# A graph network's adjacency matrix loaded in place in 1 MB transfers, its small loads in the same queue, and two pairs' first products in step

## The chip, the cores and the metric

The kernel runs on one core of a Trainium2 chip. The metric is the device time of one execution in microseconds; the kernel before takes 1300.35 us (median of 3 runs, 1299.11 to 1302.89). Engines: PE multiplies matrices, PEld loads its weights, DVE and ACT work on vectors, Pool (GpSimd) does small vector work and issues transfers, SP issues transfers. "Clock" is the share of full speed that PE was granted. Where a comparison matters it is over several executions; the two kernels' runs of one comparison alternate on one chip.

## The reference

```python
# x (8, 2048, 64), adj (2048, 2048); four layers, each x + layer(relu(layernorm(x)))
h = jnp.maximum(_layernorm(x, axis=-1), 0.0)
x = x + _L0_gnn_ref(h, adj, L0_gnn_embedding, L0_gnn_weight, L0_gnn_bias)
# ...
# _L0_gnn_ref: As = [I, A, 2 A A - I]; every A_k @ h goes through weights made from the embedding
w = jnp.einsum('nd,dkio->nkio', embedding, weight)
b = jnp.einsum('nd,do->no', embedding, bias)
# ...
x_g = jnp.einsum('knm,bmc->bnkc', A_stack, x)
out = jnp.einsum('bnki,nkio->bno', x_g, w)
return out + b
```

adj is 0 or one over the row's count, so the kernel multiplies with its signs and scales the product by a row of values taken from its diagonal (`crow`).

## The kernel before

The batch is worked in four pairs of 64 columns. The change touches the opening of layer 0. There adj comes row block by row block (16 blocks of 128 rows, "rows" from here on, 1 MB each); ACT writes the sign into `BT`, which stays in SBUF as the operand of all later products. Meanwhile the first products of pair 0 (`banks[0]`, 8 matmuls for each row) and pair 1 (`banks[1]`, 6 for each row) are accumulated. h is split into a rounded half `H` and a remainder `L`.

```python
def load_adj(m, behind):
    for nb in range(NB):                       # 4 pieces of 256 KB for each row
        part_ = slice(nb * 512, (nb + 1) * 512)
        st = prop.tile([P, 512], F32, name="st", bufs=6)
        loads.append(nc.sync.dma_start(st, adj[m * P:(m + 1) * P, part_]))
        if nb == m // 4:                       # the diagonal, picked by DVE from the staging tile
            junk = prop.tile([P, P], U8, name="junk")
            nc.vector.scalar_tensor_tensor(junk, st[...], 1.0, ident, ..., accum_out=cols[:, m, :])
        with tc.issue_after(behind.ins) if behind else nullcontext():
            nc.scalar.activation(BT[:, m, part_], st, AF.Sign)
# ... norm of one tile of x: DVE mean, z; ACT square; DVE var; Pool rstd; DVE z; ACT H; DVE L
        rstd = small.tile([P, 8], F32, name="rstd", bufs=3)
        powers.append(nc.gpsimd.tensor_tensor(rstd, var, mhalf, op=ALU.pow))
# ...
    for m in range(NCH):
        # ... tick(): the next tile's norm
        load_adj(m, copies[i - 1] if i else None)
        if len(x01) < len(norm_order):
            load_x01()                         # x, 256-byte pieces, on SP
        # ...
        last = step(0, m, banks[0])
        # ...
        while done < (m - 3 if m < 12 else 2 * m - 14):   # pair 1 three rows behind
            with tc.issue_after(last.ins):
                step(1, done, banks[1])
            done += 1
```

`issue_after` sets an instruction's place in the order of its engine; it adds no wait of its own.

## Time and profile before

| | before |
|---|---|
| time, median of 3 | 1300.35 us |
| profiled execution: span, clock | 1295.8 us, 0.979 |
| first product | 13.8 us |
| interleaved products end | 95.8 us |
| first `y` product (the next stage) | 115.2 us |
| PE busy | 95% of the span |

The prediction below shows the lines that carry its reading. Two more are needed for comparison. They are the busy time of the kernel before in two stretches of the opening: bounds in us, length, then busy us and number of instructions for PE, PEld, DVE, ACT and Pool, then clock, busy share of the transfer engines and GB/s.

```profile
30.00:38.00 8.00, 2.45 (x4) 1.01 (x4) 2.68 (x6) 2.09 (x4) 5.24 (x5) 0.50 0.77 241
38.00:47.00 9.00, 7.55 (x18) 5.15 (x18) 6.06 (x16) 5.47 (x10) 2.87 (x3) 0.57 0.57 187
```

PE ran 4 and 18 matmuls there in 8 and 9 us, at half clock, while the transfer engines were 77% and 57% busy.

### The profile page before, as it was taken

The page shows a single profiled execution, that of the slowest core. Times are in us where ns is not written, and L with a number is a line of the kernel's source. Part 1 is how long each engine was busy: PE and PEld are TensorE (multiplying, and loading weights), DVE is VectorE, ACT ScalarE, POOL GpSimd, SP SyncE. Part 2 cuts the span into 40 slices and gives each one's busy share as a digit, 9 for nine tenths or more (in the row PEclk, how much of TensorE's full clock was granted, in tenths as well). Part 3 has the DMA queues.
Part 4 walks back from the last instruction along what each step waited for, and adds up shares of the span by engine and source line. Part 5 has one row for each costly group of instructions (what it writes and reads, how often), then busy time and mean ns, then how long its engine had stood idle before and what let it go on. Part 6 is the DMA issues. An engine that isn't in the chain of part 4 may idle for free.

```text
span 1295.8 us, 15644 instructions
## 1 busy us (share of the span) xinstructions
PE 1230.5 (95%) x5702; PEld 865.2 (67%) x5702; DVE 750.2 (58%) x1937; ACT 188.6 (15%) x313; POOL 224.6 (17%) x228
## 2 busy tenths in 40 slices
PE   3799999899999999999999999999999999989994
PEld 2476555455585556655558887878878878878883
DVE  5325887777747775357764435535644544566664
ACT  4541001000010000000011121112111211111110
POOL 4210111111121111011101024004201400332222
PEclk8799999999999999989999999999999999999997
DMA  9793334322343322123237535443653463433322
GB/s 252 227 240 114 86 94 111 93 73 63 95 104 82 81 78 68 35 55 86 58 83 174 107 90 158 115 93 106 159 118 90 139 130 94 151 102 106 97 67 52
DMA packets 149882, 140.11 MB, mean 108 GB/s; under 512 B 99892, under 2 KB 101940, under 8 KB 149796
## 3 DMA queue, kind: packets, MB, share of 16 engines
q1 hardware_dynamic: 137780, 106.54, 32.1%
q0 software_dynamic: 9904, 31.96, 8.7%
q8 instruction: 47, 0.77, 0.3%
q10 hardware_dynamic: 2112, 0.52, 0.2%
q14 instruction: 39, 0.32, 0.1%
HBM read 94.87 MB, written 35.73 MB: 101 GB/s over the span
## 4 chain that ended last, share of the span: by engine, by line
PE 77%; DMA 6%; DVE 6%; issue 6%; POOL 2%; ACT 1%; SPq 1%; ACTq 0%; POOLq 0%; DVEq 0%
PE bv L217 33%; PE y L580 22%; PE bn L523 4%; PE ph L742 3%; DMA st<-in_adj_dram 2%; PE bv_2b L217 2%; PE bv_3b L217 2%; DMA hb<-hs 2%; POOL rstd L169 1%; PE bv_1b L217 1%; PE bv_0a L217 1%; PE bn_u L523 1%; PE pt L229 1%; PE bv_0b L217 1%; DVE acc L589 1%
## 5 line engine op out<-in xcount | busy, mean ns | idle before, releaser
L217 PE MATMUL bv<-BT,H 128*128 128x512 f32 x1024 | 426.7, 417 | 0.0
L217 PE MATMUL bv<-BT,L 128*128 128x512 f32 x1024 | 401.3, 392 | 0.0
L217 PEld LDWEIGHTS bv<-BT,H 128*128 128x128 f32 x1024 | 192.9, 188 | 47.9 <-issue 11.5
L217 PEld LDWEIGHTS bv<-BT,L 128*128 128x128 f32 x1024 | 193.0, 188 | 47.5 <-issue 11.5
L589 DVE SCALAR_TENSOR_TENSOR acc<-y,emb,acc 128x128 f32<-128x128 f32 x512 | 176.3, 344 | 69.2 <-PE y L580 68.4
L580 PE MATMUL y<-wt,t0T 64*128 64x512 f32 x512 | 145.7, 611 | 9.2 <-DVE odd L589 9.2
L589 DVE SCALAR_TENSOR_TENSOR odd<-y,emb,odd 128x128 f32<-128x128 f32 x448 | 153.5, 343 | 0.0
L169 POOL TENSOR_TENSOR rstd<-var,mhalf 128x8 f32<-128x8 f32 x64 | 106.1, 1660 | 197.1 <-DVE var L167 191.6
L209 DVE TENSOR_TENSOR g<-bv,crow 128x512 f32<-128x512 f32 x48 | 33.2, 692 | 182.4 <-PE bv L217 182.4
L163 ACT ACTIVATE sq<-z 128x512 f32<-128x512 f32 x64 | 40.4, 631 | 404.9 <-DVE z L159 392.8
L580 PEld LDWEIGHTS y<-wt,t0T 64*128 64x128 f32 x512 | 46.8, 186 | 72.3 <-issue 66.5
L560 POOL TENSOR_TENSOR acc<-acc,wl 128x512 f32<-128x512 f32 x16 | 21.0, 1314 | 295.2 <-DVE z L159 294.0
L561 POOL DMA_DIRECT2D xs<-acc x32 | 18.0, 562 | 284.3 <-DVE acc L597 233.7
L580 PE MATMUL y<-wt,t1T 64*128 64x512 f32 x256 | 67.0, 589 | 0.0
L172 DVE SCALAR_TENSOR_TENSOR z<-z,rstd 128x512 f32<-128x512 f32 x64 | 44.7, 703 | 35.5 <-POOL rstd L169 35.5
L523 PEld LDWEIGHTS bn<-wl,g 128*128 128x128 f32 x384 | 49.4, 191 | 6.3 <-ACT g L747 3.1
L166 DVE TENSOR_REDUCE var<-sq 128x8 f32<-128x512 f32 x64 | 43.5, 680 | 16.1 <-ACT sq L163 16.1
L523 PE MATMUL bn<-wl,g 128*128 128x128 f32 x384 | 51.2, 276 | 0.7 <-ACT H L204 0.4
L689 DVE SCALAR_TENSOR_TENSOR junk<-mt,cols,st 128x512 uint8<-128x512 bf16 x64 | 49.2, 769 | 0.8 <-DMA mt<-MD 0.3
L580 PEld LDWEIGHTS y<-wt,t1T 64*128 64x128 f32 x256 | 27.6, 187 | 27.4 <-issue 27.1
L747 ACT ACTIVATE g<-g,b1s 128x512 f32<-128x512 f32 x32 | 23.2, 724 | 139.3 <-DVE g L746 139.3
L159 DVE TENSOR_TENSOR z<-acc,mean 128x512 f32<-128x512 f32 x56 | 38.3, 691 | 6.6 <-DMA hs<-z 5.0
(208 smaller groups left out, 1694.2 us busy)
## 6 DMA issues: line engine op xcount, KB each, us to landing
st<-in_adj_dram SPq DMA_DIRECT2D x128, 256.0 KB, 4.1
crow<-crowD SPq DMA_DIRECT2D x64, 256.0 KB, 3.3
hs<-z POOLq DMA_DIRECT2D x48, 256.0 KB, 2.9
hb<-hs SPq DMA_DIRECT2D x40, 256.0 KB, 3.3
xs<-acc POOLq DMA_DIRECT2D x32, 256.0 KB, 2.4
MD<-BT POOLq DMA_DIRECT2D x16, 512.0 KB, 5.1
acc<-xs SPq DMA_DIRECT2D x32, 256.0 KB, 3.5
acc<-in_x_dram SPq DMA_DIRECT2D x48, 128.0 KB, 3.7
```

What stands on the lines that cost most here:

```text
L159: nc.vector.tensor_tensor(g, groups(xt), mean[:, :, None].to_broadcast([P, 8, C]), op=ALU.subtract)
L163: nc.scalar.activation(sq, z, AF.Square)
L166: nc.vector.tensor_reduce(var, groups(sq), axis=AX.X, op=ALU.add)
L169: powers.append(nc.gpsimd.tensor_tensor(rstd, var, mhalf, op=ALU.pow))
L172: nc.vector.scalar_tensor_tensor(groups(h), g, 0.0, rstd[:, :, None].to_broadcast([P, 8, C]), op0=ALU.max, op1=ALU.mult)
L209: ahead.append(nc.vector.tensor_tensor(out, ps, crow, op=ALU.mult))
L217: nc.tensor.matmul(ps, hl[m // 4][i][:, m % 4, :], BT[:, m, nb * 512:(nb + 1) * 512], start=(m == 0 and i == 0), stop=(m == NCH - 1 and i ...
L523: nc.tensor.matmul(ps[:, t, :], fT[:, t * P:(t + 1) * P], wmat, start=True, stop=True)
L580: nc.tensor.matmul(y[:, bb, :], terms[k][hs_, ts], wt[hs_, k, dg * 512:(dg + 1) * 512], start=(k == 0), stop=(k == K - 1),)
L589: last = nc.vector.scalar_tensor_tensor(xj, yd, ec, old, op0=ALU.mult, op1=ALU.add)
L689: nc.vector.scalar_tensor_tensor(junk, mt, cols[:, i, :], st, op0=ALU.mult, op1=ALU.not_equal, accum_out=bad[:, i, q:q + 1],)
L742: fill[12] = lambda: nc.tensor.matmul(ph, w1v2 if s else w1vT, gT[nb], start=True, stop=True)
```

## The change

The intent: the rows go as 16 transfers of 1 MB straight into `BT`, and the sign is taken in place, so no staging buffer holds the queue. Loading into `BT` must go by Pool's queue (it rounds while it copies). x and four blocks of diagonals (`dg`) go by the same queue, so that Pool's order says what comes first; stores of h go to SP. Pair 1 stays one row behind pair 0. The bias products move behind the steps. The diff also loads the weights before the first `y`, moves the first transpose of `t0` into a product and reorders the norms.

```diff
-    def load_adj(m, behind):
-        for nb in range(NB):
-            part_ = slice(nb * 512, (nb + 1) * 512)
-            st = prop.tile([P, 512], F32, name="st", bufs=6)
-            loads.append(nc.sync.dma_start(st, adj[m * P:(m + 1) * P, part_]))
...
+    def load_dg(q):
+        loads.append(nc.gpsimd.dma_start(dg[q], bass.AP(
+            tensor=adj.tensor, offset=adj.offset + 4 * q * (P * N + P),
+            ap=[[N, P], [P * N + P, 4], [1, P]],
+        )))
...
+    def load_adj(m):
+        loads.append(nc.gpsimd.dma_start(BT[:, m, :], adj[m * P:(m + 1) * P, :]))
+
+    def pool_loads(behind, what):
+
+        order.append(behind)
+        for f, i in what:
+            with tc.issue_after(order[-1].ins):
+                f(i)
+            order.append(loads[-1])
+
+    def signs(m, behind=None):
+        for hf in range(2):
+            part_ = slice(hf * (N // 2), (hf + 1) * (N // 2))
             with tc.issue_after(behind.ins) if behind else nullcontext():
-                nc.scalar.activation(BT[:, m, part_], st, AF.Sign)
+                nc.scalar.activation(BT[:, m, part_], BTf[:, m, part_], AF.Sign)
...
+    pool_loads(order[0], ((row, 0), (lx, 2), (row, 1), (lx, 3), (row, 2)))
+    tick()
+    tick()
+    plan = {
+        0: (0, ((lx, 4),)), 1: (1, ((row, 3), (lx, 5), (row, 4))),
+        2: (2, ((lx, 6), (row, 5), (lx, 7))), 3: (3, ((row, 6), (row, 7), (dia, 0), (dia, 1))),
+        4: (4, ((row, 8), (row, 9))), 6: (5, ((row, 10), (row, 11), (dia, 2), (dia, 3))),
+        8: (6, ((row, 12), (row, 13))), 10: (7, ((row, 14), (row, 15))),
+    }
     for m in range(NCH):
...
+            pool_loads(powers[plan[m][0]], plan[m][1])
...
+        signs(m, squares[m] if m in (0, 2, 3) else copies[...])
         last = step(0, m, banks[0])
...
+                last = step(1, m - 1, banks[1])
```

`plan`: row 3 and later stand on Pool behind a given rstd operation (`lx` is x of one tile, `dia` a block of diagonals).

More of the change, by code (lines that the diff above doesn't have):

```diff
@@ L112, in uniform_path @@
     mhalf = consts.tile([P, 8], F32, name="mhalf")
-    nc.vector.memset(mhalf, -0.5)
+    order = [nc.gpsimd.memset(mhalf, -0.5)]
     def part(nb):
@@ L125, in fill_x @@
             for bb in range(2):
-                queue.dma_start(
+                ld = queue.dma_start(
                     acc[:, :, bb * C:(bb + 1) * C],
@@ L129, in fill_x @@
                 )
+            return ld
         else:
@@ L148, in uniform_path @@
     pending = []
-    powers = []
+    powers, firsts, squares, lows, stored = [], [], [], [], []
     ahead = []
@@ L158, in norm_stages @@
         nc.vector.tensor_scalar(mean, mean, 1.0 / C, None, op0=ALU.mult)
-        nc.vector.tensor_tensor(
+        firsts.append(nc.vector.tensor_tensor(
             g, groups(xt), mean[:, :, None].to_broadcast([P, 8, C]), op=ALU.subtract
-        )
+        ))
         sq = block("sq", f"sq_{name}", 1)
-        nc.scalar.activation(sq, z, AF.Square)
+        squares.append(nc.scalar.activation(sq, z, AF.Square))
         yield
@@ L197, in uniform_path, with halves @@
     copies = []
-    def halves(src, name, pool=None):
+    def halves(src, name, pool=None, later=None):
         pool, bufs = (work, 6) if pool is None else (pool, 4)
@@ L204, in halves, with rest @@
         copies.append(nc.scalar.copy(Hq, src))
-        nc.vector.tensor_tensor(Lq, src, Hq.bitcast(F32), op=ALU.subtract)
+        def rest():
+            lows.append(nc.vector.tensor_tensor(Lq, src, Hq.bitcast(F32), op=ALU.subtract))
+        rest() if later is None else later.append(rest)
         return Hq, Lq
@@ L249, in done @@
         def done(z):
-            nc.gpsimd.dma_start(hs[p][:, part(nb), :], z)
+            stored.append(
+                (nc.gpsimd if xt is None else nc.sync).dma_start(hs[p][:, part(nb), :], z)
+            )
             if also is not None:
@@ L254, in norm_0 @@
         norm_relu(load_x(0, p, nb) if xt is None else xt, f"0_{p}_{nb}", done)
+    l0p = l0.enter_context(tc.tile_pool(name="l0p", bufs=1))
+    wt = l0p.tile([P, K, D * C], F32, name="wt")
     prox = pro.enter_context(tc.tile_pool(name="prox", bufs=1))
-    prop = pro.enter_context(tc.tile_pool(name="prop", bufs=1))
     emb = consts.tile([P, NCH, D], F32, name="emb")
-    norm_order = ((0, 0), (0, 1), (1, 0), (0, 2), (1, 1), (0, 3), (1, 2), (1, 3))
-    x01 = []
+    norm_order = tuple((p, nb) for nb in range(NB) for p in range(2))
+    x01, loads = [], []
     def load_x01(queue=nc.sync):
@@ L269, in load_x01, with spare, make_cols @@
             t = block("acc" if nb < 2 else "crow", nm, 2)
-        with tc.issue_after(loads[-1].ins) if loads else nullcontext():
-            fill_x(t, 0, p, nb, queue)
+        loads.append(fill_x(t, 0, p, nb, queue))
         x01.append(t)
-    loads = []
-    load_x01(nc.scalar)
-    load_x01()
-    load_x01()
+    def spare(tag, name):
+        return work.tile([P, 512], F32, tag=tag, name=name, bufs=6)
     BTf = BT.bitcast(F32)
     cols = consts.tile([P, NCH, 1], F32, name="cols")
-    def load_adj(m, behind):
-        for nb in range(NB):
-            part_ = slice(nb * 512, (nb + 1) * 512)
-            st = prop.tile([P, 512], F32, name="st", bufs=6)
-            loads.append(nc.sync.dma_start(st, adj[m * P:(m + 1) * P, part_]))
-            if nb == m // 4:
-                junk = prop.tile([P, P], U8, name="junk")
-                nc.vector.scalar_tensor_tensor(
-                    junk, st[:, (m % 4) * P:(m % 4 + 1) * P], 1.0, ident,
-                    op0=ALU.mult, op1=ALU.mult, accum_out=cols[:, m, :],
-                )
+    junk = consts.tile([P, P], U8, name="junk")
+    dg = [spare("HL"[q % 2], f"dg_{q}").rearrange("p (j n) -> p j n", j=4) for q in range(NB)]
+    def load_dg(q):
[3 more added lines that the diff above has]
+        )))
+    def make_cols(q):
+        for t in range(4):
+            nc.vector.scalar_tensor_tensor(
+                junk, dg[q][:, t, :], 1.0, ident,
+                op0=ALU.mult, op1=ALU.mult, accum_out=cols[:, 4 * q + t, :],
+            )
+    def load_adj(m):
[9 more added lines that the diff above has]
+            part_ = slice(hf * (N // 2), (hf + 1) * (N // 2))
             with tc.issue_after(behind.ins) if behind else nullcontext():
-                nc.scalar.activation(BT[:, m, part_], st, AF.Sign)
+                nc.scalar.activation(BT[:, m, part_], BTf[:, m, part_], AF.Sign)
     crows = []
@@ L304, in make_crow @@
         crows.append(crow)
-    def spare(tag, name):
-        return work.tile([P, 512], F32, tag=tag, name=name, bufs=6)
-    bd = spare("H", "bd")
-    nc.gpsimd.memset(bd, 0.0)
+    bias_tiles = []
     def bias_loads():
-        with tc.issue_after(powers[-1].ins):
-            nc.gpsimd.dma_start(emb, embedding.rearrange("(j p) d -> p j d", p=P))
-            for j in range(8):
-                nc.gpsimd.dma_start(bd[j * D:(j + 1) * D, j * C:(j + 1) * C], bias)
+        bd = spare("H", "bd")
+        nc.gpsimd.memset(bd, 0.0)
+        with tc.issue_after(stored[-1].ins):
+            nc.sync.dma_start(emb, embedding.rearrange("(j p) d -> p j d", p=P))
+        for j in range(8):
+            ld = nc.sync.dma_start(bd[j * D:(j + 1) * D, j * C:(j + 1) * C], bias)
+        bias_tiles.extend((bd, ld))
     def bias_products():
+        eT, bnb = spare("L", "embT"), (spare("H", "bnb_0"), spare("L", "bnb_1"))
+        bd = bias_tiles[0]
         pe = bank("tr", "pe")
@@ L333, in bias_products @@
             )
-    eT, bnb = spare("L", "embT"), (spare("H", "bnb_0"), spare("L", "bnb_1"))
     def back(src, p, nb):
@@ L367, in uniform_path @@
     ticks = [0]
+    rests = []
+    ticks_at = (0, 1, 2, 3, 4, 6, 8, 10)
     def tick():
         go_on()
-        if ticks[0] < len(norm_order):
-            p, nb = norm_order[ticks[0]]
-            norm_0(
-                p, nb,
-                lambda z: hls[p].append(halves(z, f"0_{p}_{nb}", prox if p else None)),
-                x01[ticks[0]],
-            )
+        while rests:
+            rests.pop()()
+        last = (lows or firsts or [None])[-1]
+        k = ticks[0]
+        if k < len(norm_order):
+            p, nb = norm_order[k]
+            with tc.issue_after(last.ins) if last else nullcontext():
+                norm_0(
+                    p, nb,
+                    lambda z: hls[p].append(
+                        halves(z, f"0_{p}_{nb}", prox if p else None, rests)
+                    ),
+                    x01[k],
+                )
+        if lows:
+            ahead.append(lows[-1])
         ticks[0] += 1
@@ L389, in uniform_path, with lx @@
     banks = [[bank(f"b{4 * p + nb}", f"bv_{p}_{nb}a") for nb in range(4 - p)] for p in range(2)]
-    for _ in range(3):
-        tick()
-    done = 0
+    load_x01(nc.scalar)
+    load_x01()
+    def lx(_):
+        load_x01(nc.gpsimd)
+    row, dia = load_adj, load_dg
+    pool_loads(order[0], ((row, 0), (lx, 2), (row, 1), (lx, 3), (row, 2)))
[7 more added lines that the diff above has]
+    }
@@ L393, in uniform_path @@
     for m in range(NCH):
-        if m in (1, 3, 5, 6, 8, 10, 12):
+        if m == 12:
+            bias_loads()
+        if m in ticks_at:
             tick()
-        i = {3: 1, 5: 2, 7: 3, 9: 4, 11: 5, 12: 6, 13: 7, 14: 8}.get(m, 0)
-        load_adj(m, copies[i - 1] if i else None)
-        if len(x01) < len(norm_order):
-            load_x01()
-        if m == 3:
-            bias_loads()
+        if m in plan:
+            pool_loads(powers[plan[m][0]], plan[m][1])
+        if m in (11, 13):
+            with tc.issue_after(lows[-1].ins):
+                for q in (0, 1) if m == 11 else (2, 3):
+                    make_cols(q)
@@ L403, in uniform_path @@
+        signs(m, squares[m] if m in (0, 2, 3) else copies[(0, 0, 1, 0, 2, 3, 4, 4, 5, 6, 7)[min(m, 10)]])
         last = step(0, m, banks[0])
-        if m == 14:
+        if m > 0:
             with tc.issue_after(last.ins):
-                for nb in range(3):
+                last = step(1, m - 1, banks[1])
+        if m in (13, 14):
+            with tc.issue_after(last.ins):
+                for nb in (0, 1) if m == 13 else (2, 3):
                     make_crow(nb)
-                bias_products()
@@ L410, in uniform_path @@
-        while done < (m - 3 if m < 12 else 2 * m - 14):
-            with tc.issue_after(last.ins):
-                step(1, done, banks[1])
-            done += 1
-    make_crow(3)
+    with tc.issue_after(last.ins):
+        step(1, NCH - 1, banks[1])
+        bias_products()
+    for k in range(K):
+        for hf in range(2):
+            with tc.issue_after(bias_tiles[1].ins):
+                wt_load = nc.sync.dma_start(
+                    wt[hf * C:(hf + 1) * C, k, :].rearrange("i (d o) -> i d o", d=D),
+                    weight[:, k].rearrange("d i o -> i d o"),
+                )
@@ L443, in uniform_path @@
     nc.gpsimd.dma_start(t1D[:, 3 * 512:], tx)
+    with tc.issue_after(lows[-1].ins):
+        nc.vector.tensor_tensor(wt[:, 0, :], wt[:, 0, :], wt[:, 2, :], op=ALU.subtract)
+        nc.vector.tensor_scalar(wt[:, 2, :], wt[:, 2, :], 2.0, None, op0=ALU.mult)
     ahead.clear()
@@ L464, in col @@
         for hf in range(2):
-            nc.sync.dma_start(t[hf * C:(hf + 1) * C, :], src)
+            with tc.issue_after(wt_load.ins):
+                nc.sync.dma_start(t[hf * C:(hf + 1) * C, :], src)
         return t
@@ L502, in make_weights @@
         for hf in range(2):
-            nc.sync.dma_start(ivt[:, hf * C:(hf + 1) * C], iv)
+            with tc.issue_after(wt_load.ins):
+                nc.sync.dma_start(ivt[:, hf * C:(hf + 1) * C], iv)
         nc.gpsimd.dma_start(wD[:, 0:4], tr)
@@ L542, in prepare_next @@
         hl.append(halves(h, nm))
-    l0p = l0.enter_context(tc.tile_pool(name="l0p", bufs=1))
-    wt = l0p.tile([P, K, D * C], F32, name="wt")
-    for k in range(K):
-        for hf in range(2):
-            nc.sync.dma_start(
-                wt[hf * C:(hf + 1) * C, k, :].rearrange("i (d o) -> i d o", d=D),
-                weight[:, k].rearrange("d i o -> i d o"),
-            )
-    nc.vector.tensor_tensor(wt[:, 0, :], wt[:, 0, :], wt[:, 2, :], op=ALU.subtract)
-    nc.vector.tensor_scalar(wt[:, 2, :], wt[:, 2, :], 2.0, None, op0=ALU.mult)
     def keep(p, nb, acc, name, more=None):
@@ L602, in feat_0 @@
         return to_feat(h, term(0, f"t0T_{p}_{q}"), f"0_{p}_{q}")
-    t0T = feat_0(0, 0)
+    first_t0 = []
     for p in range(NP):
@@ L632, in uniform_path @@
                 hl1, nb, nm, term(2, f"t2T_{nm}"), crow,
-                fill={8: lambda: prepare(2)} if nb == 3 else {},
-            )
+                fill={8: lambda: prepare(2)} if nb == 3
+                else {12: lambda: first_t0.append(feat_0(0, 0))} if p + nb == 0 else {},
+            )
+            if p + nb == 0:
+                t0T = first_t0[0]
             go_on()
```

## The prediction

> **What bounds the kernel now.** I read the page's slices first, then busy time by stretch, the waits, the transfer queue's own waits and the chain of the first 120 us. The page shows where PE is not full:
>
> ```profile
> PE   3799999899999999999999999999999999989994
> DVE  5325887777747775357764435535644544566664
> ACT  4541001000010000000011121112111211111110
> PEclk8799999999999999989999999999999999999997
> DMA  9793334322343322123237535443653463433322
> ```
>
> A slice is 32.4 us. PE is busy 90% and more nearly everywhere; only the first two slices (3 and 7) leave much, at a granted clock of 8 and 7 tenths, with DMA at 9, 7, 9. The change touches only this opening, in which adj is loaded and the first products of pairs 0 and 1 are made, so all it can win lies ahead of about 106 us. The busy time by stretch splits it (columns: stretch, length, busy PE, PEld, DVE, ACT, POOL, clock, DMA share, GB/s):
>
> ```profile
> 6.00:8.00 2.00, 0.00 (x0) 0.00 (x0) 1.97 (x6) 0.40 (x1) 0.00 (x0) 1.00 1.03 373
> ...
> 13.80:46.00 32.20, 20.64 (x47) 12.77 (x48) 19.60 (x47) 16.59 (x30) 19.23 (x22) 0.68 0.79 235
> 46.00:85.30 39.30, 36.59 (x153) 27.18 (x152) 5.86 (x28) 26.59 (x44) 2.27 (x2) 1.00 0.84 265
> 60.00:80.00 20.00, 19.96 (x85) 15.16 (x84) 1.53 (x12) 15.30 (x25) 0.00 (x0) 1.00 0.90 301
> 85.30:95.80 10.50, 10.34 (x46) 6.91 (x46) 5.99 (x10) 0.21 (x1) 2.63 (x5) 1.00 1.06 167
> 95.80:106.30 10.50, 9.57 (x52) 7.44 (x51) 6.13 (x11) 2.35 (x4) 2.16 (x4) 1.00 0.45 148
> ```
>
> From 13.8 to 46 us PE ran only 47 matmuls while DMA moved 235 GB/s, against the 373 it reached at 6 to 8 us. The waits say why:
>
> ```profile
> PE bv_0a L383 <- ACT H L204: 13.8, 1, 13.8
> ...
> PEld bv_3a L383 <- ACT BT L294: 8.4, 6, 4.2
> ...
> PEld bv_0a L383 <- ACT BT L294: 7.1, 5, 3.1
> ```
>
> PE waits for ACT's sign of an adj block, and ACT for the block. The transfer queue's own waits:
>
> ```profile
> SPq L286 <- ACT BT L294: 27.1, 39, 4.2
> ...
> SPq L286 <- DVE junk L289: 13.6, 9, 3.2
> ```
>
> The queue stood 41 us because its six staging buffers of 256 KB were still to be read by ACT or by DVE's diagonal pick: a circle of load, sign, free, load. So the chain is full of it:
>
> ```profile
> 51.85 4.37 DMA st<-in_adj_dram
> 56.24 0.64 ACT BT L294
> 56.90 4.72 DMA st<-in_adj_dram
> ```
>
> The last adj block's sign ends at 85.5 us; pair 1 lags behind pair 0, and the interleaved products end at 95.8.
>
> **What the Trainium skill says.** (1) "DMA: Bandwidth & Descriptors", section "Measured (HBM→SBUF, 128 partitions, SWDGE, issued from GpSimd)", gives 341 GB/s for a lone 1 MB load and 425 for 16 MB. This trace has no such load, but 373 GB/s in 2 KB pieces fits. (2) The same page, "SWDGE vs HWDGE vs iDMA": a load into a float32r tile always casts, and only GpSimd can issue one. That is why loading in place needs the Pool queue; the trace's one cast transfer, MD (1 MB read, 512 KB written), lands in 5.1 us, so casting is not slow. (3) "TensorE: Matmul & The Clock Gate", section "What's actually happening": after an idle window of about 3.4 us PE falls to half clock. The trace agrees: clock 0.68 in the starved stretch, matmuls 0.43 us apart there against 0.23 later. (4) "SBUF — State Buffer", section "Who interferes with whom": DVE's two-port modes keep GpSimd from writing descriptors. No wait here shows it.
>
> **The change, part by part.**
> Removed: 64 loads of 256 KB through six buffers, and both buffer waits. Added: 16 loads of 1 MB straight into the place of the operand, and 4 diagonal loads of 256 KB. The order of instructions shows the Pool queue with row 0, x, row 1, x, row 2 at once; the rest is let go behind the eight rstd operations, each issue also waiting for the transfer eight before it, which still leaves several MB in flight.
> ACT: 64 signs (0.54 us apart back to back) become 32 of double width, about 1.08 us each by that spacing: 35 us either way, off the path.
> Pool: some 32 issues at about 0.6 us (the hs issue's mean) and 8 rstd at 1.7: 33 us of work, enough room in 50 us. It loses hs stores to SP.
> DMA, new bound: adj 16.8 MB, x 2.1, diagonals 1.05, hs stores 2.1, together 22 MB. With 301 and 373 GB/s as the two ends of what was seen, I choose 335: 66 us. From 2.1 us that is 68; I add 1.5 for landing and 1.5 for short gaps where loads stand behind an rstd: row 15 is in place at about 71 us, against about 84.9 before.
> PE, other bound: x of the first tile now shares the engines with row 0, so I let the first matmul slip from 13.8 to about 14.5. 224 matmuls at 0.232 us are 52 us, four crow transposes 1.8, cold start about 3: 71 us. The two bounds lie together, which is why neither can be had whole.
> After row 15: sign of the first half 1.1, then 20 matmuls (8 of pair 0, 12 of pair 1) 4.6, two late crow transposes 0.9: products end at about 77.5 instead of 95.8, a gain of 18.
> Given back: bias products (0.29 + 0.94 + 0.98 in the chain) move from before that point to after it: minus 2.2. The 32 matmuls of the last block of pair 1 and four transposes stay, 9.2 us. The weights' load (1.6 MB in 256 B pieces) can now run beside the last rows; I charge 0.5 us. The t0 transpose moved inside the product saves the 0.9 us gap ahead of it at most.
> Sum: 18.3 − 2.2 − 0.5 + 0.9 = 16.5 us; everything after is the same program shifted, so 1300.35 − 16.5 = 1283.9. I predict **1284**.
>
> **Rivals.**
> A. DMA runs at 373 or better and PE warms early: the PE bound, 71, plus the last matmuls unhidden, 72.5: gain about 22, 1278. For it: large pieces and no buffer waits. Against: 256 B pieces of x, a diagonal load in 512 B pieces, and rows let go behind rstd.
> B. The single queue becomes a new wait: Pool's rstd, stuck behind an issue that waits for a slot, delays a norm, which delays the loads behind it; or x's small pieces come late beside 1 MB rows. For it: the chain already gives rstd 9.8% of the first 120 us. Then products end near 84 to 88: gain 7 to 10, 1291.
> C. The loads are hidden anyway. Against: between 13.8 and 85.5 us PE ran 200 matmuls, 46 us of full-speed work, in 72 us, and the waits name the blocks. Little chance.
> D. PE stays at half clock because each 1 MB row comes at once with gaps between. Half clock makes 14 matmuls last 6 us, longer than a row's 3 to 4, so PE would be full and warm again; I give it 1 to 3 us.
>
> **Range and chances.** A and B bound it: 1277 to 1292. Faster by 2% needs 26 us, so products done by 68, below the PE bound of 71: 5%. Slower by 2% needs a stall that no part adds: 1%. Within 2%: 94%.
>
> **What would show it.** Right: no wait of the load queue on ACT; GB/s over 300 from 30 us to the end of the rows; sign of row 15 near 71; pair 1 one row behind pair 0, with the interleaved products ending at 75 to 80; first `y` product near 98 instead of 115. B shows as PE or DVE waits on rstd or x between 15 and 35 us, and DMA share under 0.7 there. A shows as PE full from 20 us on with clock 1.00. If the time after the first `y` differs by over 3 us from before, the claim that the rest is only shifted is wrong.

## The result, and the profile after

In the first comparison the changed kernel took 1294.56 us (median of 4, 1292.47 to 1296.9) and the kernel before 1300.59 (median of 4). The ratio is 0.9953, 95% interval 0.993 to 0.9975. Ratios here and below are the mean time of one kernel's fast runs over that of the other's fast runs of the same rounds, so they are not quite the ratio of the medians. A second comparison of five rounds gave 1292.96 against 1301.44, ratio 0.9932 (0.9917 to 0.9947). So the gain is 6 to 8.5 us, where 16.5 were predicted, and the time lies outside the predicted range.

| profiled execution | before | after | predicted for after |
|---|---|---|---|
| span | 1295.8 us | 1292.9 us | |
| first product | 13.8 | 15.0 | 14.5 |
| sign of row 15 starts | 85 | 71.9 | 71 |
| interleaved products end | 95.8 | 81.9 | 77.5 |
| first `y` product | 115.2 | 103.4 | 98 |
| from the first `y` to the end | 1180.7 | 1189.5 | as before |

The slices of the page after, which answer to those in the prediction:

```profile
PE   4899999999999999989999999999999999899993
...
PEclk9999999999999999989999999999999999999996
DMA  8982443233232222132256525433553552523321
```

PE's first two slices went from 3 and 7 to 4 and 8, the clock there from 8 and 7 to 9 and 9. In the other 38 slices hardly a digit of PE differs; the loss after the opening sits in a few spots that a slice of 32 us does not show.

Busy time by stretch after, the same stretches as in the prediction:

```profile
13.80:46.00 32.20, 24.42 (x85) 17.92 (x86) 16.93 (x34) 18.51 (x23) 20.17 (x22) 0.95 0.93 303
46.00:85.30 39.30, 38.21 (x170) 29.80 (x170) 19.52 (x57) 19.27 (x22) 12.71 (x19) 0.99 0.95 272
```

PE has 85 matmuls where it had 47 from 13.8 to 46 us, at clock 0.95 and not 0.68, and the transfers run at 303 GB/s and not 235. The load queue's waits on ACT and on DVE's diagonal pick are gone. What ended the waits of the engines in the first 105 us (us in total, times, longest):

```profile
ACT BT L318 <- DMA BT<-in_adj_dram: 18.6, 10, 3.8
...
POOL rstd L170 <- DVE mean L159: 10.1, 1, 10.1
...
PE bv_0a L417 <- ACT BT L318: 6.3, 4, 2.4
```

ACT now waits for the rows themselves, and there is a new line: Pool stood 10.1 us in one piece before an rstd. In finer stretches:

```profile
30.00:38.00 8.00, 4.87 (x18) 3.09 (x19) 2.75 (x7) 4.37 (x6) 7.15 (x8) 1.00 0.94 305
38.00:47.00 9.00, 6.63 (x23) 5.04 (x22) 3.45 (x7) 4.49 (x7) 0.22 (x1) 0.81 1.07 397
47.00:52.00 5.00, 5.00 (x24) 4.12 (x23) 3.81 (x8) 3.64 (x6) 3.68 (x5) 1.00 0.57 158
...
56.00:66.00 10.00, 8.92 (x38) 6.37 (x36) 5.10 (x33) 5.76 (x6) 1.02 (x2) 1.00 1.12 404
```

The transfers move 397 to 404 GB/s when rows are queued, but 305 from 30 to 38 us and 158 from 47 to 52, where the engines are 57% busy. The reason is in the order of Pool's instructions (start, length, line, operation, tiles, idle time before it and what ended it):

```profile
37.07 1.16 POOL L304 DMA_DIRECT2D BT<-in_adj_dram  x2
48.32 1.67 POOL L170 TENSOR_TENSOR rstd<-var,mhalf 128x8 f32<-128x8 f32 x1 [10.10 <-DVE mean L159]
49.95 0.58 POOL L304 DMA_DIRECT2D BT<-in_adj_dram  x1
```

Rows 8 and 9 were issued at 37.07, rows 10 and 11 only at 49.95, behind an rstd that could not start before 48.32. Why it was late is in ACT's order:

```profile
41.91 2.00 ACT L318 ACTIVATE BT<-BT 128x1024 fp32r<-128x1024 f32 x2 [3.82 <-DMA BT<-in_adj_dram]
44.61 1.06 ACT L318 ACTIVATE BT<-BT 128x1024 fp32r<-128x1024 f32 x1 [0.70 <-DMA BT<-in_adj_dram]
45.58 0.60 ACT L205 CAST H<-z 128x512 fp32r<-128x512 f32 x1
46.09 0.63 ACT L164 ACTIVATE sq<-z 128x512 f32<-128x512 f32 x1
```

The cast at 45.58 had its input from DVE at 40.0 (`z`, 39.34 + 0.69), but stood behind the signs of rows 6 and 7, which waited 3.82 and 0.70 us for their rows. The remainder, the square and the variance follow it, then the rstd, then the rows. This is a circle: rows wait on Pool for an rstd, the rstd waits through DVE for a cast on ACT, and the cast waits behind a sign for a row.

### The profile page after: what moved, and what is told of

Same layout as the page of the kernel before. It is cut to its first block, busy times and chain, and to the rows that moved or that the text cites.

```text
span 1292.9 us, 15524 instructions
## 1 busy us (share of the span) xinstructions
PE 1225.3 (95%) x5702; PEld 865.0 (67%) x5702; DVE 751.6 (58%) x1936; ACT 182.4 (14%) x281; POOL 236.8 (18%) x244
## 4 chain that ended last, share of the span: by engine, by line
PE 75%; issue 8%; DMA 6%; DVE 6%; POOL 2%; SPq 1%; ACT 1%; ACTq 0%; POOLq 0%; DVEq 0%
PE bv L221 33%; PE y L628 20%; PE bn L583 4%; PE ph L793 3%; PE bv_2b L221 2%; DMA BT<-in_adj_dram 2%; PE bv_3b L221 2%; POOL rstd L170 1%; DMA hb<-hs 1%; PE bv_1b L221 1%; PE bv_0a L221 1%; PE bv_0b L221 1%; PE bn_u L583 1%; DVE acc L637 1%; PE pS L838 1%
```

## The experiments

Two theories for the opening, which is 4.4 us short of the prediction. "Circle": the late rstd that holds rows 10 to 15 is the loss. "Early rows": the loss is PE's waits on rows 3 to 6 between 26 and 43 us. Two for the 8.8 us lost after the first `y`: chance of the execution, or something that the change does every time. Two terms of this section: the drain is the longest of Pool's DRAIN instructions on the program's last line; the late store is the ninth store of `xs` on Pool, which starts 1.97 us after the sum that it stores.

### Both kernels once more

No edit.

> The kernel before once more, for its profile. Theory 'chance': the losses that the changed kernel showed after its first y (4 us between 419 and 450 us at a half clock from 415.1 to 421.9 us, and 3.5 us in the Pool drain at the end, 5.62 against 1.54 us) are placed anew in each execution; then this profile has its half-clock stretches after 100 us at other times than 571-585 us, or its last Pool drain well above 1.54 us. Theory 'systematic': half clock again at 571-585 us for about 13.7 us and the drain again at 1.5 us, within 0.3 us.

> The changed kernel once more. Ratio to before expected 0.9953 again (0.993 to 0.9975), so about 1294.5 us. Theory 'chance' for what is lost after the first y: the half clock at 415-422 us or the 5.6 us drain moves or shrinks in this profile while the opening (row 15's sign near 72 us, first y at 103.5 us) stays within 0.5 us. Theory 'systematic': both come back at the same place and size, drain 5.4 to 5.8 us, half clock 415-422 us.

Measured: before again 1300.51 us (a single run); half clock at 575.2 to 588.8 us, drain 1.54 us. After again 1292.96; drain 5.62 us, half clock at 416.6 to 420.1 (3.4 us where it was 6.8), first `y` at 102.8. From the first `y` to the end, before took 1180.7 and 1181.8 us, after 1189.5 and 1189.1. The loss comes back, 8.8 and then 7.3 us, and so does the drain: it is systematic in size. The half-clock stretches shift by a few us and change their lengths.

### Rows 10 and 11 released one rstd earlier (e_release)

```diff
-        4: (4, ((row, 8), (row, 9))), 6: (5, ((row, 10), (row, 11), (dia, 2), (dia, 3))),
+        4: (4, ((row, 8), (row, 9), (row, 10), (row, 11))), 6: (5, ((dia, 2), (dia, 3))),
```

> Rows 10 and 11 issued on Pool right after rows 8 and 9 (near 38.5 us, not 49.95). Theory 'circle' (the opening is short because rows 10 to 15 wait on a late rstd): the hole in the transfers at 47-52 us closes (DMA share 0.57 goes above 0.9), rows 12 to 15 land 2 to 3 us earlier, products end 3 to 4 us earlier (78 to 79 us, not 82.1), time 1290 to 1292. Rival 'early rows' (the TensorE waits at 26-43 us, on rows 3 to 6, are what is lost, and these come at 250 to 305 GB/s): the hole closes but only the two waits near 65 us (0.88 and 0.21 us) go; products end near 81 us, time within 1.5 us of the changed kernel.

Measured: 1289.01 us, ratio to before 0.9904 (0.989 to 0.9919); products end at 78.3 us, first `y` at 99.8.

```profile
47.00:52.00 5.00, 4.60 (x20) 3.15 (x19) 2.29 (x5) 4.20 (x6) 4.59 (x5) 1.00 1.07 419
```

The hole is closed: 419 GB/s where 158 stood. The products end 3.6 us earlier than in the first profile of the changed kernel (3.0 than in the second, 81.3), as the circle theory said; the rival's 81 was not met, and the time is below both forecasts. PE's waits in the middle also shrank, since row 6's sign came at 39.9 us and not at 41.6 to 41.9. Row 6 stands ahead of the edit in Pool's order, and in e_lag, with the old plan, its sign came at 39.6: this share, up to 2.4 us of PE's waits, is not shown to be the edit's.

### All rows from 3 on, and late x, released earlier (e_flow)

```diff
-    pool_loads(order[0], ((row, 0), (lx, 2), (row, 1), (lx, 3), (row, 2)))
+    pool_loads(order[0], ((row, 0), (lx, 2), (row, 1), (lx, 3), (row, 2), (lx, 4), (row, 3), (lx, 5)))
...
+        0: (0, ((row, 4),)), 1: (1, ((lx, 6), (row, 5))),
+        2: (2, ((lx, 7), (row, 6))), 3: (3, ((row, 7), (row, 8), (dia, 0), (dia, 1))),
+        4: (4, ((row, 9), (row, 10), (row, 11))), 6: (5, ((row, 12), (row, 13), (dia, 2), (dia, 3))),
+        8: (6, ((row, 14), (row, 15))),
```

> Every row from 3 on, and x of the later tiles, released one to two rstd operations earlier, so that the transfer queue isn't empty between 15 and 56 us. Theory 'early rows': the waits of TensorE on rows 3 to 6 (0.73, 0.75, 0.22, 2.28 and 2.37 us) shrink by 4 us or more, row 15's sign starts at 66 to 69 us and not 72, products end at 76 to 78.5 us and the first y near 98 us; time 1288 to 1290.5. Theory 'circle': no more than e_release brings. Theory 'rows are bound by the transfer rate itself': rows 5 and 6 land within 1 us of 35.6 and 41.9 us as before, no gain.

Measured: 1285.43 us, ratio 0.987 (0.9856 to 0.9884), less than forecast; the profile is of the slowest of its four runs, 1290.02 us. Row 15's sign starts at 65.6 us, products end at 74.7, first `y` at 97.8.

```profile
15.00:30.00 15.00, 12.67 (x49) 10.36 (x50) 11.58 (x23) 11.96 (x15) 11.43 (x12) 1.00 1.00 325
30.00:38.00 8.00, 7.39 (x33) 5.74 (x31) 4.45 (x10) 4.82 (x7) 5.58 (x6) 1.00 1.01 348
47.00:52.00 5.00, 4.30 (x18) 2.95 (x17) 3.45 (x13) 4.71 (x6) 3.01 (x4) 1.00 1.07 421
```

With the same bytes the transfers now move 325 GB/s from 15 to 30 us (257 in the changed kernel), 348 from 30 to 38 (305) and 421 from 47 to 52 (158), so the rate itself did not bind them. From its first product to 85 us PE waits 1.3 us in all, where the changed kernel's first profile shows 7.7. So both theories hold in part: the order of release is worth 7.2 us at the products' end (81.9 to 74.7), more than the 4.4 that were short, and e_release alone brings 3.6 of them. The prediction's products at 77.5 us and first `y` at 98 were reachable with this data, but not with this `plan`. The first product came late, at 17.3 us: x issues stood ahead of the first rstd and waited for a transfer eight before them.

### Pair 1 three rows behind again, in the changed kernel (e_lag)

```diff
...
-        if m > 0:
-            with tc.issue_after(last.ins):
-                last = step(1, m - 1, banks[1])
+        while done < (m - 3 if m < 12 else 2 * m - 14):
+            with tc.issue_after(last.ins):
+                last = step(1, done, banks[1])
+            done += 1
...
```

> The changed kernel with the second pair three rows behind as before, to see what 'both pairs in step' is worth by itself. My prediction's sum has the row waits hidden behind nothing in either order. Theory 'waits in the middle add to what is left after them': the same waits on rows 3 to 6 and 12, and more left after row 12 (two more rows of 6 products, 2.6 us), products end 2 to 4 us later than 82.1, time 1294 to 1297 (changed kernel 1293 beside it). Rival 'the backlog fills the waits': products end within 1 us of 82.1.

Measured: 1296.6 us, ratio 0.9968 (0.9937 to 0.9999); products end at 85.5 us, 3.6 later than in the changed kernel's first profile. That is what "both pairs in step" is worth here with the clock included: this profile ran at half clock from 26.2 to 36.4 us, the other for 3.4 us, and I did not separate the two. The interval of the time overlaps the changed kernel's. The rival is out: a backlog of pair 1 did not fill PE's waits, which came to 8.6 us; in PE's order it stands behind the same row.

### 15 more small transfers on Pool, in the kernel before (b_pool15)

The changed kernel issues 135 transfers on Pool, before 120. This and the next run ask whether the number makes the long end.

```diff
+    for k in range(15):
+        scr = dram.tile([P, 8], F32, name=f"scr{k}")
+        nc.gpsimd.dma_start(scr, ones[:, 8 * k:8 * k + 8])
```

> The kernel before with 15 small extra transfers issued on Pool in its first microseconds (135 on Pool and not 120, as in the changed kernel), nothing else. In all four profiles of the changed kernel and its variants the last Pool drain takes 5.62 us and the operation ahead of it 1.54 us, in both profiles of before 1.54 and 0.56; and the ninth store of xs starts 1.97 us after its sum where all others take 0.3. Theory 'number of Pool transfers': here too the drain is near 5.6 us and one store of a z or acc tile starts 1.7 us late; time 3 to 6 us longer than before. Rival 'their bytes or the adjacency in place': drain 1.54, no late store, time within 2 us of before.

Measured: 1294.58 us, ratio 0.997 (0.9942 to 0.9999); drain 2.76 us, no late ninth store. Neither theory: the drain grew by 1.22 us, 0.08 for each small transfer. (The opening became 3.6 us shorter, first `y` at 111.6, though the first rstd came later. I did not follow that up.) A store of `xs` is late here too, but the 21st, at 878.7 us.

### x of the last four tiles and the diagonals on SP (e_flow_sp)

```diff
-        loads.append(nc.gpsimd.dma_start(dg[q], bass.AP(
+        loads.append(nc.sync.dma_start(dg[q], bass.AP(
...
+    pool_loads(order[0], (..., (row, 2), (row, 3), (row, 4)))
+    for _ in range(4):
+        load_x01()          # on SP
...
```

The rows of `plan` also stand one place earlier than in e_flow.

> As e_flow, with x of the last four tiles and the diagonal blocks on SP's queue (123 transfers on Pool and not 135), so that Pool is free for the first rstd operations, and rows one slot earlier still. Theory 'number of Pool transfers': last drain below 3 us, late ninth store of xs gone or elsewhere, the part after the first y 3 to 9 us shorter than e_flow's 1190.5. First y at 95 to 98 us (e_flow 97.8) unless the 256-byte pieces of x starve beside the rows, then 100 to 104. Time 1279 to 1283 if both hold; 1285 if the end stays as it was.

Measured: 1288.8 us, ratio 0.9912 (0.989 to 0.9933). The drain fell to 2.03 us, the ninth store is on time (the 26th is late), and the time after the first `y` is 1182.6 us, 8 less than in e_flow. But the first `y` came at 104.8 and the time missed its forecast, for a reason that one line of DVE's timeline shows:

```profile
33.65 0.69 DVE L160 TENSOR_TENSOR z<-x,mean 128x512 f32<-128x512 f32 x1 [13.32 <-DMA hs<-z]
```

DVE waited 13.32 us for a store of h, which stood in SP's queue behind x. In the records of the single pieces from 13 to 25 us, Pool's queue moved 640 (7,335 bytes in the mean) and SP's 641 (247 bytes): one for one, in every 3 us of it too, so x got 13.2 KB a us beside 391 KB a us of rows. The Trainium skill, "DMA: Bandwidth & Descriptors", section "Queues, rings and completion order", says that each transfer engine goes round robin between its queues packet by packet, several pieces to a packet. The equal counts agree with the turns; how many pieces a turn takes they do not show. They show what it means when the pieces differ thirtyfold. This is what the change's single queue avoids.

### Diagonals on ACT, x on Pool (e_flow_dg); all of x first, on ACT and SP (e_xfirst)

```diff
+        loads.append(nc.scalar.dma_start(dg[q], bass.AP(      # both
...
+    pool_loads(order[0], (..., (row, 2), (lx, 4), (row, 3)))   # e_flow_dg: 131 transfers on Pool
+    pool_loads(order[0], ((row, 0),))                          # e_xfirst: 119, none of x
```

> As e_flow, with x of tile 5 behind the first two rstd operations, and the four diagonal blocks (2,048 pieces of 512 bytes) in ACT's queue from the start: 131 transfers on Pool and not 135, no diagonal blocks among them. Question 1, the opening: first product at 15 to 15.6 us (e_flow 17.33, where rstd stood behind the x issues), first y at 95.5 to 97.5. Question 2, what makes the last Pool drain (1.54 before, 2.76 with 15 small transfers more, 2.03 with 123, 5.62 with 135) and the late ninth store of xs: if it is the diagonal blocks, drain near 2 and no late store, time 1279 to 1282; if it is x, drain still above 4.5 and the late store there, time 1283 to 1286.

> All of x first, by ACT's and SP's queues, row 0 on Pool from the start and rows 1 to 15 after the first rstd; diagonal blocks on ACT behind x: 119 transfers on Pool. In e_flow_sp x crawled at about 12 KB a us in 256-byte pieces beside 384 KB a us of rows; here only row 0 is beside it. Theory 'a queue of small pieces gets one piece for each 8 KB piece of a row': x complete by 16 us, rows from then on at 2.6 to 2.9 us each, PE waits once for row 1 (2 to 4 us), first y 96 to 99 us. Theory 'Pool transfers of x and of the diagonal blocks make the late store and the long drain': drain 1.5 to 2.1 us, no late store of xs in layer 0, the part after the first y at 1180 to 1183 us (before 1180.7, changed kernel 1189.5). Time 1277 to 1281; without the second theory 1284 to 1288.

Measured: e_flow_dg 1287.52 us, ratio 0.9893 (0.9876 to 0.9909), drain 4.48, no late store; first product at 18.1 and first `y` at 98.6. Its opening missed what I expected: x came 0.85 us later than in e_flow, and the four issues of diagonals held ACT, whose first square ran at 13.3 us with its input ready at 10.1. After the first `y` it took 1188.7 us, nearly as long as the changed kernel, without the ninth store being late; the section on the prediction's error says where that went. e_xfirst 1286.02 us, ratio 0.9888 (0.9871 to 0.9904); drain 0.89, no late store, 1179.7 us after the first `y`: its tail was even a little shorter than expected. Its opening did not: ACT's twelve issues held ACT's first square until 16.8 us, the first product came at 21.6 and the first `y` at 103.6.

Put side by side, the drains of the changed kernel's family go by the number of transfers of 512 pieces on Pool (x: 256-byte pieces; diagonals: 512-byte pieces): none 0.89 us, 4 of them 2.03, 12 of them 4.48, 16 of them 5.62. That is 0.29, 0.31 and 0.29 us for each.

### The same in the kernel before: 8 transfers of 512 pieces (b_pieces8)

```diff
+    for k in range(8):
+        scr = dram.tile([512, 32], F32, name=f"scr{k}")
+        nc.gpsimd.dma_start(scr.rearrange("(j p) c -> p j c", p=P), ones.rearrange("p (j c) -> p j c", j=4))
```

> The kernel before with 8 small extra transfers on Pool at its start, each in 512 pieces of 128 bytes (64 KB in all eight of them 512 KB), nothing else. Theory 'the last Pool drain goes by the number of pieces issued on Pool over the whole run, whatever their bytes': from 0.285 to 0.306 us for each transfer of 512 pieces, the drain is 1.54 + 8 x 0.30 = 3.9 us (3.6 to 4.2), and the operation ahead of it 0.56 + 8 x 0.074 = 1.15 us. Rival 'it goes by transfers': 8 x 0.081 = 0.65, drain 2.2 us. Rival 'by bytes or by loads into SBUF': drain 1.5 to 1.6 us.

Measured (a single run, so its 1297.03 us decides nothing): drain 3.91 us, the operation ahead of it 1.13. These are the instructions of the program's last line, with shortest, middle and longest duration in ns and the first and last start. The kernel before:

```profile
L1439 POOLq DRAIN  x3: 46/107/1538, 1293.4 to 1295.5; - x3
```

With 8 transfers of 512 pieces added, 64 KB each:

```profile
L1445 POOLq DRAIN  x3: 46/107/3907, 1290.5 to 1295.0; - x3
```

The changed kernel:

```profile
L1490 POOLq DRAIN  x3: 46/107/5622, 1286.4 to 1292.6; - x3
```

The forecast of 3.9 us was met, and both rivals (2.2 and 1.5) are out: pieces count, not transfers and not bytes into SBUF. The 15 transfers of b_pool15, in 128 pieces each, fit: 0.08 us is about a quarter of 0.30. Count the pieces of all issues on Pool (the shape stands in each record) and 16 more for each transfer (the records have that many 4-byte pieces, 1,920 for 120 transfers and 2,160 for 135): the count is 17,456 in e_gate, 18,624 before, 25,904 in the changed kernel, and in all 14 profiles the drain lies within 0.05 us of one straight line, 0.89 us at 17,456 and 0.56 more for each thousand. The Trainium skill, "VectorE: DVE Perf Modes", section "The DRAIN you can't avoid", knows two kinds, one after each DVE operation and one of the runtime's own, constant at about 12 ns on all engines; Pool's last one, 0.89 to 5.62 us here, is neither. Not all of it shows in the span: from Pool's last output issue to the end, before takes 8.28 us, b_pieces8 9.84, the changed kernel 11.76, so of 4.1 us more of drain the changed kernel pays 3.5.

### A version that takes the parts that paid (e_gate, e_gate2)

e_gate has the rows in place, the pairs in step, no x and no diagonals on Pool, and holds row 0 until x of tile 4 has landed, so that x does not starve.

```diff
+    load_x01(nc.scalar)
+    for _ in range(7):
+        load_x01()
+    gate = consts.tile([P, 8], F32, name="gate")
+    gated = nc.gpsimd.tensor_tensor(gate, x01[4][:, 0, C:C + 8], mhalf, op=ALU.add)
...
+    pool_loads(gated, ((row, 0), (row, 1)))
...
+        0: (0, ((row, 2),)), 1: (1, ((row, 3), (row, 4))),
+        2: (2, ((row, 5), (row, 6))), 3: (3, ((row, 7), (row, 8))),
+        4: (4, ((row, 9), (row, 10), (row, 11))), 6: (5, ((row, 12), (row, 13))),
+        8: (6, ((row, 14), (row, 15))),
```

> e_xfirst mended: all of x by ACT's and SP's queues, row 0 held on Pool until x of tile 4 has landed (a small sum on Pool reads it), rows 0 and 1 ahead of the first rstd, the diagonal blocks in ACT's queue after the second square and not before the first: 119 transfers on Pool. In e_xfirst ACT's issues held its first square until 16.8 us and row 0 held x; the first product came at 21.59 us. Theory: x complete at 11 to 12 us, first product at 14.5 to 16.5 us, PE waits under 2 us in the steps, first y 95 to 98.5 us; and the tail as in e_xfirst, where the last Pool drain goes by the pieces issued on Pool (0.89 us with none of x or of the diagonal blocks; about 0.29 us for each 512-piece transfer over 0.89, 2.03, 4.48 and 5.62 us), so 1180 to 1182 us after the first y. Time 1279 to 1282, the best of all. Rival: something else than the pieces makes the tail, drain above 2 us; or x starves again beside the rows, first y above 101 us and time 1285 to 1287.

Measured: **1278.78 us** (1277.35 to 1280.55), ratio to before 0.9844 (0.9828 to 0.9861); its output agrees with the reference. It is 21 us under the kernel before and, with an interval that lies wholly below, under the changed kernel's 0.9932 (0.9917 to 0.9947), each against the kernel before of its own rounds. First `y` at 97.8 us; drain 0.89 us; 1177.5 us after the first `y`, 2.5 less than the least that was expected, which I have not traced.

```profile
15.00:30.00 15.00, 9.91 (x37) 8.13 (x38) 7.44 (x15) 10.66 (x14) 4.44 (x5) 1.00 1.03 385
...
38.00:47.00 9.00, 8.40 (x37) 6.47 (x36) 6.75 (x14) 7.75 (x10) 5.79 (x6) 1.00 1.08 410
```

Another expectation failed: the first product came at 20.1 us and not at 14.5 to 16.5, because the diagonals ran ahead of row 0 and the first cast stood behind its sign. PE made up for it with 0.8 us of waits in the steps. e_gate2 moves both.

```diff
-    for q in range(NB):
-        with tc.issue_after(squares[1].ins):
-            load_dg(q)
...
+        if m == 0:
+            for q in range(NB):
+                with tc.issue_after(squares[2].ins):
+                    load_dg(q)
...
-        signs(m, squares[m] if m in (0, 2, 3) else copies[...])
+        signs(m, squares[m] if m in (2, 3) else copies[...])
```

> e_gate with two changes in order: the diagonal blocks are asked for after the third square and not the second (in e_gate they took 206 KB a us at 11 to 13 us, ahead of row 0, whose sign came at 17.53 us), and the first H cast stands ahead of row 0's sign on ACT (it was ready at 13.4 us and ran at 19.4). Theory: row 0's sign at 14.5 to 16 us, first product at 16 to 18 us (20.09), first y at 94.5 to 96.5 us (97.79), time 1275.5 to 1278. Rival: the four issues (2.6 us of ACT) and the 512-byte pieces only move: row 1 or the diagonals come late, first y within 1 us of 97.8, time 1278 to 1280. Tail 0.89 us either way.

Measured: 1280.64 us, ratio 0.9855 (0.9831 to 0.9879). The first product came at 15.8, but PE then waited 2.3 us for row 1 and the first `y` came at 98.2: the rival's case, the issues only moved. The intervals of the two overlap almost wholly, so neither is shown to be better.

Not tried on the chip: rows in place from SP's queue. The builder refuses it ("only gpsimd can initiate dmas that cast"), and with a plain float32 view of `BT` as the target it does not compile. Not tried either: larger transfers or more staging buffers in the kernel before. So what size and place of the loads are each worth is not separated.

## Why the prediction was wrong

**Right.** The buffer waits went, rows in place came when said (row 15's sign at 71.9 us, predicted 71), and pair 1 keeps one row behind. Between the products' end and the first `y`, 2.1 us were given back (19.4 us before, 21.5 after); the sum had 2.2 + 0.5 - 0.9 = 1.8.

**Wrong, first step: "the two bounds lie together", taken as 71 us for each, with 77.5 as the end.** Both bounds were about right by themselves (row 15 came at 71.9 us; in e_flow PE took 56.0 us from its first product to its last without its waits, where the sum had 56.8), yet the products ended at 81.9. A bound on the last row and a bound on PE's work give only the later of two ends when PE never waits on the way. PE did wait: in the changed kernel's first profile 7.7 us from 26 to 66 us, and 3.4 us of the steps ran at half clock. The last wait was for row 12, at 66.0 us; from there PE was full to the end. A row of work for PE takes 14 matmuls of 0.232 us, 3.25 us, and the last rows came faster than that (1.05 MB at 404 GB/s, 2.6 us), so whatever PE lost before row 12 could no longer be hidden. Rival B (a queue held by an rstd) was half right, with the products' end at 84 to 88 us: loads did stand behind a late rstd. But it had the rstd stuck behind an issue without a free slot, where it waited for DVE and, through it, for a cast on ACT; and it looked between 15 and 35 us, where the hole lay at 47 to 52. In the sum it stood only as "1.5 for short gaps where loads stand behind an rstd". e_release and e_flow measure it: the products end at 78.3 and 74.7 us when the same loads are released earlier.

**Wrong, second step: "everything after is the same program shifted".** By its own test (over 3 us) it failed: 1180.7 us before, 1189.5 after. PE has the same 5,368 matmuls from the first `y` on in both, so they can be matched one by one. Three parts add up to 8.8 us.
- At the end, 3.5 us: the last Pool drain, 5.62 us instead of 1.54. Shown: it goes by the pieces issued on Pool, and the change put 16 transfers of 512 pieces there.
- About 311 us after the first `y`, 4.0 us. PE's timeline there, before:

```profile
426.08 1.13 PE L580 MATMUL y<-wt,t0T 64*128 64x512 f32 x4 [1.91 <-DVE odd L589]
```

and after:

```profile
415.81 1.23 PE L628 MATMUL y<-wt,t0T 64*128 64x512 f32 x2 [2.91 <-DVE odd L637]
```

The wait is 1.0 us longer, and the clock fell to half within it, from 415.1 to 421.9 us, which cost 3.0 more. The wait is longer because of the late store; the other fourteen of the first fifteen take 0.3 us, and the loads that follow it on SP came later by as much. It is in all five profiles with 16 transfers of 512 pieces on Pool, where this wait of PE was 2.72 to 3.12 us; in the nine others the ninth store is on time and the wait was 1.18 to 2.01. What decides where a late start falls can be read from the traces. With the count of the drain (pieces, and 16 for each transfer) every one of the 14 profiles has a late start on Pool, at the transfer with which the count passes a value between 16,352 and 16,400. In the kernel before it is a store of h at 1036.9 us (2.79 us after its input, where 0.3 is usual), in b_pieces8 the fifteenth store of `xs` (2.30), in b_pool15 the 21st, and in e_flow_sp the 26th:

```profile
1001.55 0.61 POOL L612 DMA_DIRECT2D xs<-acc  x1 [2.71 <-issue]
```

The same store in the changed kernel:

```profile
998.07 0.60 POOL L609 DMA_DIRECT2D xs<-acc  x1 [0.30 <-POOL acc L608]
```

So the change did not make the late start; its pieces moved it to a store on which PE waits. In e_flow_dg it falls on a store of weights at 569.5 us, and there that kernel lost 3.9 us against before, with 1.7 more at the wait of this bullet, by the clock alone. What happens at that count no run shows. How a wait tips the clock is not a simple threshold either: 2.0 us left it full in the second profile of before, 1.89 did not in e_flow_dg.
- Some 1.3 us elsewhere, 0.5 of it before that place, which I have not traced.

**How the range failed.** It held the opening's rivals only. The opening alone (first `y` 11.8 us earlier) would have given 1288.8, inside 1277 to 1292; the loss of the second step put it outside.

Of the places in the skill: rows back to back came at 404 GB/s, between the page's figures for 1 MB and 16 MB, so (1) agrees. (2) agrees: rows in place did not build on another queue. For (3), half clock came in pieces of 3.4 us and its multiples, as the page's window has it (all but the last, which the end of the record cuts). But it set in during shorter waits: the half clock that the prediction read as agreement began in the kernel before at 21.8 us, within a wait of 1.9 us.

## What to carry to other kernels

Where an engine consumes what a queue delivers, sum its waits from the first to the last delivery; the later of two bounds is only a floor. When transfers and the arithmetic that lets them go share one in-order engine, release them as early as the memory allows, and look for a circle through the other engines' orders. Count the pieces that a change puts on Pool, not only the bytes: they were paid for at the end, 0.3 us for each 512; and small pieces beside large ones starved when their queues were served piece for piece, so give them the engines first or put them in the same queue.

## What the Trainium skill lacked or had wrong

- "VectorE: DVE Perf Modes", section "The DRAIN you can't avoid": of the two kinds of drain that it names neither is Pool's on the program's last line. That took 0.89 us with no 512-piece transfer of the opening on Pool, 2.03 with 4, 4.48 with 12, 5.62 with 16; 8 added to the kernel before took it from 1.54 to 3.91. No page has that the end grows with the pieces issued on Pool.
- "DMA: Bandwidth & Descriptors", section "Queues, rings and completion order": turn by turn fits (640 against 641 pieces in 12 us), but the page does not draw the consequence: a queue of 256-byte pieces moved 13.2 KB a us beside one of 8 KB pieces with 391, and DVE waited 13.3 us for a store behind it.
- No page names the late start of a Pool transfer: in each of 14 profiles one, some 1.7 to 3 us later than usual, where the count of pieces and 16 for each transfer passes a value between 16,352 and 16,400.
- "TensorE: Matmul & The Clock Gate", section "What's actually happening", speaks of idle windows of about 3.4 us. Here the clock fell to half at waits of 1.89 and 2.91 us inside busy work, and at one of 2.0 it did not.
